# Reordering sums in a ring of buffers, moving a bias product into the first attention, and halving the last image's z: attention plus a non-local block on one Trainium2 core

## The chip, the core and the metric

The kernel runs on one core of a Trainium2 chip. The metric is device time in microseconds (us), the median over runs of the same program. Five engines work side by side, each through its own instructions in order: TensorE (PE in the profile, its weight loads PEld), VectorE (DVE), ScalarE (ACT), GpSimd (POOL) and SyncE (SP), which here only issues DMAs. They wait for one another through semaphores.

## The reference

The input x is 8 images of 512 channels and 32 x 32 positions, float32. The first layer is self-attention over positions with 8 heads of 64 channels and a residual; the second is a non-local block without a softmax, then a normalization over images and positions.

```python
# layer 0, per image: 512 channels, N = 1024 positions, 8 heads, d = 64
q, k, v = Wq@x + bq, Wk@x + bk, Wv@x + bv
attn = softmax(q_h^T k_h * d**-0.5)           # per head h
x1 = x + Wp@(attn v) + bp
# layer 1, C_INTER = 256
f = (theta@x1 + theta_b)(phi@x1 + phi_b)^T / N # 256 x 256
z = W@(f @ (g@x1 + g_b)) + W_b + x1
out = (z - mean) * rsqrt(var + eps) * gamma + beta   # over images and positions
```

Because the rows of a softmax add up to 1, the bias of v can be added after the projection: the kernel adds Wp@bv to bp once, and never to v.

## The kernel before

Channels lie on the 128 partitions in CC = 4 chunks, positions along the free axis, in float32 throughout. All projections are products of 2 x 2 blocks done with seven block products in place of eight (`seven`, L258; the table `SEVEN`, L220). For that, four differences of the data are needed per operand, named t1 to t4 (`more_sums`, L197), and four sums of the weights (`weight_sums`, L103). For q and k of images 1 to 7, and for the projection by Wp of images 1 to 6, some of the seven products are themselves done in seven smaller ones (`nested`, L240). Those need second-level differences of 128 x 256, held in one block per operand (`inner_parts`, L207): "inner 21" and "inner 22" from quarters of the data, "inner t4" from t4. For q and k they are used in the order 21, t4, 22 (L243, L244). The partial results of the smaller products sit in PSUM tiles named pq_in_s, pk_in_s, pp_in_s, which VectorE adds to the result (L319). TensorE accumulates the next small product on the same PSUM region, so it must wait for that addition.

A product with inner ones runs through numbered units, one 128 x 512 matmul each (16 of them in q and k). After a unit, `fills[unit]` calls a function of the caller (L303); so the caller places VectorE's work at points of TensorE's order. Instructions given to `dve`, `pe` or `sp` keep the program's order on their engine. All others are placed by a scheduler, which may move them ahead as far as their data and buffers allow.

Per image b the main loop (L801) runs: attention of image b; q, v and k of image b + 1, in this order; the projection by Wp of image b; theta and phi; then f, g, wf and z of the second layer. In the attention, scores are made 128 keys by 512 queries for two heads at once (L456), exponentiated by ScalarE into blocks e (L459), multiplied with v (L482) and added up by VectorE for the denominators (L465). `near_end` (L807) is called two steps before its end and prepares the differences of the next image's x. The denominators are folded together by DMAs that accumulate (`together`, L492) in a tile `fold` of 4 x 1024 per partition, then finished by a matmul, `den`, and a reciprocal (`all_denominators`, L520), after the second product of v (L836).

One ring of ten blocks of 128 x 1024 (`block`, L76) holds the e blocks, all differences t and inner blocks, and some weights. A new block can be written only when the last reader of the old one there is done. So the order in which blocks are asked for decides which old block each one waits for. In the phase of k, the differences of o (the attention's output) for the projection by Wp are made at `fills` 5, 7, 11 and 12, and its inner 21 at 13 and 14 (L840 to L843).

For image 0, `join_bias` (L174) makes Wp@bv: GpSimd scales and adds the quarters of Wp in SBUF after they are loaded, and four matmuls of one column (`pbp`, L187) add them over partitions, just before the projection.

z of the last three images (LATE = 3) is left for the end, because the statistics need all images. `last_z` (L747) goes over the four channel chunks oc. In each, `late_unit` (L726) makes z of an image for 1024 positions (4 matmuls), adds it to x1 and takes its statistics (`bn_stats`, L741), in two halves of 512 only for the last image of the last chunk. Then `begin` and `finish` aggregate the chunk's statistics, and all 8 images' chunk is normalized by ScalarE (in the last chunk by VectorE too) and written out by DMAs of 512 KB (L774). For chunk 0, z of the other late images was made earlier, so one image, number 7, is left.

Of the kernel before, what the change touches and what calls it, by code (L numbers as in the profile page):

```python
# [8 lines left out]
F32 = mybir.dt.float32  # L9
I32 = mybir.dt.int32  # L10
AF = mybir.ActivationFunctionType
ALU = mybir.AluOpType
# [4 lines left out]
P = 128  # L17
# [13 lines left out]
def unshifted(ctx: ExitStack, tc: tile.TileContext, a: dict, out: bass.AP):  # L31
    nc = tc.nc
    B, C, H, W = a["x"].shape
    N = H * W
    CC = C // P
# [26 lines left out]
    def pe(ins):  # L62
        tc.keep_in_program_order(ins)
# [8 lines left out]
    def next_bank(name):  # L72
        free.append(free.pop(0))
        return bank(free[-1], name)

    def block(name):  # L76
        return ring.tile([P, 2, 512], F32, tag="e", name=name)
# [93 lines left out]
        nc.sync.dma_start(kept[name][:, :14 * w.shape[3]], w.rearrange("p i k f -> p (i k f)"))  # L171
        nc.sync.dma_start(kept[name][:, 14 * w.shape[3]:], rest[name][:, :wide])

    def join_bias(w):  # L174

        t = w3.tile([P, 2, 512], F32, tag="acc", name="wp_bv")
        half = C // 2
        for m, quarters in enumerate(((w[:, 0], w[:, 1]), (corner["WpT"], w[:, 2]))):
            to, one = (t[:, i, m * half:(m + 1) * half] for i in range(2))
            for c in range(CC):  # L180
                nc.gpsimd.tensor_scalar(one if c else to, quarters[c // 2][:, c % 2, :], bv[:, c:c + 1], 1.0,
                                        ALU.mult, ALU.mult)
                if c:
                    nc.gpsimd.tensor_tensor(to, to, one, ALU.add)
        ps = next_bank("pbp")[:, 0, :CC]
        for oc in range(CC):
            pe(nc.tensor.matmul(ps[:, oc:oc + 1], t[:, 0, oc * P:(oc + 1) * P], ones, start=True, stop=True,  # L187
                                skip_group_check=True))
        nc.vector.tensor_tensor(bp, bp, ps, ALU.add)

# [6 lines left out]
    def more_sums(data, which, pin=lambda ins: None):  # L197
        for i in which:
            l, r = {1: ("12", "11"), 2: ("22", "t1"), 3: ("22", "12"), 4: ("21", "t2")}[i]
            data[f"t{i}"] = block(f"t{i}_{data['name']}")  # L200
            pin(nc.vector.tensor_tensor(data[f"t{i}"], data[l], data[r], ALU.subtract))

    def inner_sums(data, which, pin=lambda ins: None):
# [226 lines left out]
    def attention(b, q, k, v, near_end, make_f=None):  # L430
# [88 lines left out]

        def all_denominators(ps):  # L520

            t = folded.pop("t")[:, 2, :]
            columns(ps, folds8, lambda j: t[:, j * 512:(j + 1) * 512])
            ri = t[:, :512]
            nc.vector.reciprocal(ri, ps)
            d = dram2.tile([16, 512], F32, tag="den", name=f"den_d_{b}")
            nc.sync.dma_start(d, ri.rearrange("(a s) n -> a s n", a=16)[:, 0, :])
            d = d.rearrange("(j g i) n -> g j (i n)", j=2, g=2)
            return d[0], d[1]
# [36 lines left out]
        for i in range(len(steps) + LAG):  # L566
            if i < len(steps):
                scores(i)
            if make_f and i == 2:
                make_f(bank(tags[2], f"pf_{b - 1}"))  # L570
            if i in ((len(steps) - 5, len(steps) - 3) if make_f else (len(steps) - 2,)):
                near_end()
            if i >= LAG:
                weighted(i - LAG)
            if make_f and i == 46:
                first_den = denominators(0, bank(tags[2], f"den_{b}_0")[:, 0, :])
        free[:] = tags
# [169 lines left out]
    def last_z():  # L747
        order = [B - LATE, B - 1, *range(B - LATE + 1, B - 1)]
        for oc in range(CC):
            for n, b in enumerate(order if oc else [B - 1]):  # L750
                for h0, h1 in ((0, 1), (1, 2)) if (oc, n) == (CC - 1, LATE - 1) else ((0, NH),):
                    late_unit(b, oc, h0, h1)
            finish(oc, *begin(oc))

# [46 lines left out]
    for b in range(B):  # L801
        last = b == B - 1
        nxt = {}
        if not last:
            nxt["x"] = load_x(b + 1)

        def near_end():  # L807
            if not last:
                nxt["data"] = data_sums(quarters_of(nxt["x"]), f"x_{b + 1}", (1, 2))
                inner_sums(nxt["data"], "22", dve)  # L810
            elif "data" not in nxt:
                nxt["data"] = data_sums(quarters_of(held["x"]), f"x1_{b - 1}_again", (1,))
            elif "t2" not in nxt["data"]:
                more_sums(nxt["data"], (2,))
            else:
                more_sums(nxt["data"], (3, 4), dve)

        def held_f(ps):
            held["f"] = make_f(b - 1, held["tp"], ps)

        o, denominators, normalize = attention(b, q, k, v, near_end, held_f if last else None)
        between = None
        if not last:
            inner_sums(nxt["data"], "21", dve)
            later, of_t4 = [], []
            fills = {4: lambda: more_sums(nxt["data"], (3,), dve),
                     5: lambda: (more_sums(nxt["data"], (4,), dve), of_t4.extend(inner_parts(nxt["data"], "t4", dve))),
                     6: lambda: (of_t4[0](), of_t4[1]()), 7: lambda: (of_t4[2](), of_t4[3]())}
            q, peak_q = heads_of(b + 1, "q", weights("WqT"), bq, nxt["data"], dve, inner="WqT",
                                 later=later, fills=fills)  # L830
            load_w(nc.sync)

            def norm():
                nxt["products"] = normalize(denominators(next_bank(f"den_{b}")[:, 0, :]))

            v = values(b + 1, weights("WvT"), nxt["data"], {1: norm, 2: lambda: [one() for one in later], 5: lambda: nxt["products"]()})  # L836
            load_w(nc.sync)

            nxt["o"], of_21 = data_sums(quarters_of(o), f"o_{b}", ()), []
            fills = {unit: lambda i=i: more_sums(nxt["o"], (i,), dve) for unit, i in ((5, 1), (7, 2), (11, 3), (12, 4))}  # L840
            if b:
                fills[13] = lambda: (of_21.extend(inner_parts(nxt["o"], "21", dve)), of_21[0](), of_21[1]())
                fills[14] = lambda: (of_21[2](), of_21[3]())  # L843
            later_k = []
            k, peak_k = heads_of(b + 1, "k", weights("WkT"), bk, nxt["data"], later=later_k, inner="WkT",
                                 fills=fills)
            if b:
                inner_sums(nxt["o"], "t4", dve)
            load_w(nc.sync)
        else:  # L850
            nonlocal_(b - 1, held["x"], nxt["data"], held["f"], weights("WgT"), lambda: None,
                      {3: lambda: nxt.update(d=denominators(next_bank(f"den_{b}_1")[:, 0, :]))})
            z[b - 1] = [held["x"][:, cc, :] for cc in range(CC)]
            between = {4: late_unit(b - 1, 0, sums_now=False)}
            normalize(nxt["d"])()
            load_w(nc.sync)
            put_away(b - 1)
            for i, tag in enumerate("vqk"):
                reload(i, mats, tag)
            reload(3, foldp, "fold")  # L860
        w = weights("WpT")
        if b == 0:
            join_bias(w)
        project(b, xt, o, w, between, nxt.get("o"))
        if b == 0:
            keep_inner("WpT", w)
        load_w(nc.sync)
        if b == B - LATE:
            for cc in range(CC):
                nc.sync.dma_start(spill[b][:, cc, :], xt[:, cc, :])  # L870
        data = data_sums(quarters_of(xt), f"x1_{b}", (1, 2, 3, 4) if last else (1, 2))
        if last:
            reload_chunks(B - LATE)
        elif b > B - LATE and b != B - 2:
            z[b] = [xt[:, cc, :] for cc in range(CC)]
        tp = theta_phi(b, weights("tp"), data, {} if last else
                       {1: lambda: [one() for one in later_k[:2]], 2: lambda: [one() for one in later_k[2:]],
                        4: lambda: bound_scores(b + 1, q, k, peak_q, peak_k)})
        load_w(nc.sync)

        def before_wf():
            if last:
                late_unit(B - LATE, 0)
                z[b] = [xt[:, cc, :] for cc in range(CC)]
                reload(4, mats, "o")
                take_back(B - LATE + 1)

        if last:
            take_back(B - LATE)
        if b == B - 2:  # L890
            held.update(x=xt, tp=tp)
        else:
            nonlocal_(b, xt, data, lambda ps: make_f(b, tp, ps), weights("WgT"), before_wf)
            load_w(nc.sync)
            if b in spill_g:
                put_away(b)
        xt = nxt.get("x")
# [221 lines left out]
```

## Time and profile before

| what | value |
|---|---|
| median of 4 runs | 2154.0 us (2153.84 to 2154.33) |
| the profiled execution, its own time | 2154.0 us |
| its span, first to last instruction | 2152.3 us |
| granted TensorE clock | 0.996 |
| TensorE matmul busy | 2126.3 us, 99% of the span |
| VectorE busy | 1398.8 us, 65% |
| ScalarE busy | 746.4 us, 35% |
| GpSimd busy | 205.1 us, 10% |
| attention of image 0 begins, of image 1, of image 2 | 78.8, 345.8, 609.9 us |
| last matmul of the last z | about 2131 us |

The page lists, for each engine, its busy time, and for each group of instructions the line of the kernel, what it writes and reads, its count, and the mean duration of one. The chain of waits goes back from the last instruction to what released each step. The timeline lists instructions in order of time, merged where like ones follow each other, with the idle time ahead of them and what ended it. A matmul of 128 x 512 in float32 is two entries, and starts 0.86 us before the next one; the durations in the entries overlap, so starts are compared with starts.

### The profile page before, as it was taken

How to read it: one execution, taken by the hardware profiler on the slowest of the kernel's cores; microseconds unless marked ns; L12 is line 12 of the kernel's file. 1: busy time of each engine (PE TensorE's matmuls, PEld its weight loads, DVE VectorE, ACT ScalarE, POOL GpSimd, SP SyncE). 2: the span in 40 equal slices, each digit the busy share in tenths (PEclk: the TensorE clock that was granted, in tenths of full speed). 3: DMA queues.
4: the chain of work that ended last, by engine and by line, in shares of the span. 5: the costliest groups of instructions: out<-in, count | busy, mean ns of one | idle time of the engine just before them, and what ended most of it. 6: DMA issues, size and time to landing. Idle time of an engine off the chain costs nothing.

```text
span 2152.3 us, 30084 instructions
## 1 busy us (share of the span) xinstructions
PE 2126.3 (99%) x12510; PEld 1121.7 (52%) x12510; DVE 1398.8 (65%) x1690; ACT 746.4 (35%) x854; POOL 205.1 (10%) x256
## 2 busy tenths in 40 slices
PE   9999999999999999999999999999999999999996
PEld 4534664356733567335663366633666347643462
DVE  6466756667576675766657666576674675756736
ACT  1464104641046310463105621056212652056116
POOL 0111100110001100011000100011000110001000
PEclk9999999999999999999999999999999999999998
DMA  6333443334143331433324342233434234122758
GB/s 221 136 47 61 142 155 125 50 70 129 72 130 48 80 116 72 133 50 81 109 95 115 48 100 96 99 106 50 107 139 151 40 48 139 52 60 38 225 199 340
DMA packets 53375, 229.97 MB, mean 107 GB/s; under 512 B 9712, under 2 KB 16112, under 8 KB 45680
## 3 DMA queue, kind: packets, MB, share of 16 engines
q1 hardware_dynamic: 41552, 198.21, 27.2%
q0 software_dynamic: 10192, 28.46, 11.0%
q8 instruction: 100, 1.64, 0.3%
q10 hardware_dynamic: 1488, 1.32, 0.2%
q14 instruction: 43, 0.35, 0.1%
HBM read 140.79 MB, written 46.27 MB: 87 GB/s over the span
## 4 chain that ended last, share of the span: by engine, by line
PE 94%; DVE 2%; ACT 1%; DMA 1%; issue 1%; DVEq 0%; ACTq 0%
PE ps L456 20%; PE po L482 20%; PE pv L295 9%; PE ptp L295 9%; PE pp L295 7%; PE pq L295 5%; PE pg L295 4%; PE pk L295 4%; PE pq_in_s L250 3%; PE pf L622 3%; PE pz L295 2%; PE pk_in_s L250 2%; PE pp_in_s L250 2%; PE pwf L657 1%; DVE k L319 1%; ACT z L773 1%
## 5 line engine op out<-in xcount | busy, mean ns | idle before, releaser
L459 ACT ACTIVATE e<-ps 128x1024 f32<-128x1024 f32 x512 | 522.8, 1025 | 432.2 <-PE ps L456 426.7
L465 DVE TENSOR_TENSOR acc<-acc,e 128x1024 f32<-128x1024 f32 x384 | 469.9, 1224 | 144.6 <-ACT e L459 141.3
L482 PE MATMUL po<-e,v 64*64 64x512 f32 x4096 | 528.7, 589 | 0.7 <-ACT w_WgT L624 0.7
L456 PE MATMUL ps<-q,k 64*64 64x512 f32 x4096 | 529.1, 589 | 0.0
L482 PEld LDWEIGHTS po<-e,v 64*64 64x64 f32 x4096 | 156.5, 133 | 283.4 <-issue 275.7
L456 PEld LDWEIGHTS ps<-q,k 64*64 64x64 f32 x4096 | 155.6, 133 | 284.1 <-issue 275.0
L495 POOL DMA_DIRECT2D fold<-acc x189 | 147.2, 779 | 984.4 <-DMA fold<-acc 574.6
L463 DVE TENSOR_TENSOR acc<-e,e 128x1024 f32<-128x1024 f32 x64 | 78.3, 1224 | 143.7 <-ACT e L459 143.7
L645 ACT ACTIVATE g<-pg,gb 128x512 f32<-128x512 f32 x31 | 21.3, 687 | 410.6 <-PE pg L295 410.5
L295 PE MATMUL pv<-w_WvT,t_x 128*128 128x256 f32 x512 | 116.4, 381 | 0.0
L295 PE MATMUL ptp<-w_tp,t_x 128*128 128x256 f32 x512 | 114.4, 379 | 0.0
L295 PEld LDWEIGHTS pv<-w_WvT,t_x 128*128 128x128 f32 x512 | 96.6, 190 | 18.5 <-issue 5.7
L411 ACT COPY v<-pv 128x1024 f32<-128x1024 f32 x32 | 32.4, 1013 | 212.8 <-PE pv L295 212.8
L295 PEld LDWEIGHTS ptp<-w_tp,t_x 128*128 128x128 f32 x512 | 97.3, 190 | 13.2
L295 PE MATMUL pp<-t_o,w_WpT 128*128 128x512 f32 x208 | 100.8, 592 | 0.0
L295 PE MATMUL pq<-t_x,w_WqT 128*128 128x512 f32 x200 | 99.9, 593 | 0.6 <-DVE w_WqT L784 0.6
L423 POOL TENSOR_SCALAR q<-q,gates 128x1024 f32<-128x1024 f32 x32 | 35.2, 1113 | 680.5 <-DVE gates L421 587.3
L295 PE MATMUL pk<-t_x,w_WkT 128*128 128x512 f32 x200 | 100.0, 592 | 0.0
L295 PE MATMUL ptp<-w_tp,x 128*128 128x256 f32 x384 | 87.4, 381 | 0.0
L295 PE MATMUL pv<-w_WvT,x 128*128 128x256 f32 x384 | 86.8, 379 | 0.0
L319 DVE TENSOR_TENSOR k<-k,pk_in_s 128x256 f32<-128x256 f32 x119 | 48.3, 419 | 55.9 <-PE pk_in_s L250 41.5
L319 DVE TENSOR_TENSOR q<-q,pq_in_s 128x256 f32<-128x256 f32 x119 | 48.5, 420 | 51.1 <-PE pq_in_s L250 48.4
(179 smaller groups left out, 2306.4 us busy)
## 6 DMA issues: line engine op xcount, KB each, us to landing
fold<-acc POOLq DMA_DIRECT2D x189, 128.0 KB, 3.1
w_WqT<-kept_WqT SPq DMA_DIRECT2D x7, 2368.0 KB, 8.8
w_WkT<-kept_WkT SPq DMA_DIRECT2D x7, 2368.0 KB, 8.9
r<-den_d SPq DMA_DIRECT2D x32, 512.0 KB, 7.2
x<-in_x_dram SPq DMA_DIRECT2D x31, 512.0 KB, 5.8
w_WpT<-kept_WpT SPq DMA_DIRECT2D x6, 2176.0 KB, 8.3
w_WvT<-kept_WvT SPq DMA_DIRECT2D x7, 1792.0 KB, 7.1
w_tp<-kept_tp SPq DMA_DIRECT2D x7, 1792.0 KB, 7.3
```

Source lines behind the costliest of these rows:

```text
L250: pe(nc.tensor.matmul(ps, a[wi], d[di], start=s not in begun, stop=True, skip_group_check=True))
L295: pe(nc.tensor.matmul(to_ps, lhsT(k), rhs(k), start=(s, at) not in begun, stop=(k == nk - 1), skip_group_check=True))
L319: pin(nc.vector.tensor_tensor(at, at, ps if len(ps.shape) == 3 else ps.unsqueeze(1), ALU.add))
L411: seven(f"pv_{b}", w, data, True, lambda q, ps: nc.scalar.copy(at(q), as_v(ps)), lambda q, ps: dve(nc.vector.tensor_tensor(at(q), at(q), a ...
L423: nc.gpsimd.tensor_scalar(q[:, p, :], q[:, p, :], gate[:, p:p + 1], 1.0, ALU.mult, ALU.mult)
L456: pe(nc.tensor.matmul(ps[c * P // 2:(c + 1) * P // 2, j, :], k[r, p, keys], q[r, p, h * 512:(h + 1) * 512], start=True, stop=True, skip_gr ...
L459: nc.scalar.activation(e, ps, AF.Exp, scale=SCALE)
L463: nc.vector.tensor_tensor(accs[u], es[u, 0], e, ALU.add)
L465: ins = nc.vector.tensor_tensor(accs[u], accs[u], e, ALU.add)
L482: pe(nc.tensor.matmul(ps[j * D:(j + 1) * D, r, :], v[keys, m, (2 * p + j) * D:(2 * p + j + 1) * D], e[keys, j, :], start=(m == 0), stop=(m ...
L495: nc.gpsimd.dma_start(to, part_of, accum_op=ALU.add)
L622: pe(nc.tensor.matmul(ps[:, c, :], tp[:, i, c * P:(c + 1) * P], tp[:, i, CI:], start=(i == 0), stop=(i == NB - 1)))
```

## The change

Three parts.

1. Ring order. `near_end` asks for the block of t2 before that of t1, and makes inner 21 of the next x there instead of inner 22. Inner 22 is made in the phase of q, at units 8 and 9, its block asked for at unit 4. In the phase of k, t3 and t4 of o move from units 11 and 12 to 10 and 11, and its inner 21 from 13 and 14 to 12 and 14.
2. Bias. `join_bias` no longer takes the loaded quarters of Wp. It loads the four chunks of Wp anew into the unused fourth part of the tile `fold` of image 0's attention, by four DMAs on SP's queue, and VectorE scales and adds them, one `tensor_scalar` and three `scalar_tensor_tensor` of 128 x 512. None of the eight is pinned to an order. The four matmuls of one column stand just ahead of `den` of image 0, in the other half of its PSUM tile.
3. Last z. In `last_z`, the last image of every chunk is made in two halves of 512 positions; in chunk 0 that is image 7, the only one.

```diff
-    def join_bias(w):
-
-        t = w3.tile([P, 2, 512], F32, tag="acc", name="wp_bv")
-        half = C // 2
-        for m, quarters in enumerate(((w[:, 0], w[:, 1]), (corner["WpT"], w[:, 2]))):
-            to, one = (t[:, i, m * half:(m + 1) * half] for i in range(2))
-            for c in range(CC):
-                nc.gpsimd.tensor_scalar(one if c else to, quarters[c // 2][:, c % 2, :], bv[:, c:c + 1], 1.0,
-                                        ALU.mult, ALU.mult)
-                if c:
-                    nc.gpsimd.tensor_tensor(to, to, one, ALU.add)
-        ps = next_bank("pbp")[:, 0, :CC]
+    def join_bias(t):
+
+        t = t.rearrange("p (a n) -> p a n", a=2)
+
+        def get(c, to):
+            return lambda: nc.sync.dma_start(t[:, to, :], turned["WpT"][:, c, :])
+
+        def more(c):
+            return lambda: nc.vector.scalar_tensor_tensor(t[:, 0], t[:, 1], bv[:, c:c + 1], t[:, 0], ALU.mult, ALU.add)
+
+        return {9: get(0, 0), 10: get(1, 1), 14: lambda: nc.vector.tensor_scalar(t[:, 0], t[:, 0], bv[:, 0:1], 1.0,
+                                                                               ALU.mult, ALU.mult),
+                15: more(1), 17: get(2, 1), 22: more(2), 25: get(3, 1), 30: more(3)}
+
+    def bias_product(t, ps):
         for oc in range(CC):
-            pe(nc.tensor.matmul(ps[:, oc:oc + 1], t[:, 0, oc * P:(oc + 1) * P], ones, start=True, stop=True,
+            pe(nc.tensor.matmul(ps[:, oc:oc + 1], t[:, oc * P:(oc + 1) * P], ones, start=True, stop=True,
                                 skip_group_check=True))
         nc.vector.tensor_tensor(bp, bp, ps, ALU.add)
...
-            t = folded.pop("t")[:, 2, :]
+            t = folded.pop("t")
+            if b == 0:
+                bias_product(t[:, 3, :], ps[:, 1, :CC])
+            t, ps = t[:, 2, :], ps[:, 0, :]
...
+            if b == 0 and i == 8:
+                aside = join_bias(folded["t"][:, 3, :])
+            if b == 0 and i > 8 and i in aside:
+                aside[i]()
...
-            for n, b in enumerate(order if oc else [B - 1]):
-                for h0, h1 in ((0, 1), (1, 2)) if (oc, n) == (CC - 1, LATE - 1) else ((0, NH),):
+            images = order if oc else [B - 1]
+            for b in images:
+                for h0, h1 in ((0, 1), (1, 2)) if b == images[-1] else ((0, NH),):
...
-                nxt["data"] = data_sums(quarters_of(nxt["x"]), f"x_{b + 1}", (1, 2))
-                inner_sums(nxt["data"], "22", dve)
+                nxt["data"] = data_sums(quarters_of(nxt["x"]), f"x_{b + 1}", ())
+                nxt["data"]["t2"] = block(f"t2_x_{b + 1}")
+                more_sums(nxt["data"], (1, 2))
+                inner_sums(nxt["data"], "21", dve)
...
-            inner_sums(nxt["data"], "21", dve)
-            later, of_t4 = [], []
-            fills = {4: lambda: more_sums(nxt["data"], (3,), dve),
+            later, of_22, of_t4 = [], [], []
+            fills = {4: lambda: (of_22.extend(inner_parts(nxt["data"], "22", dve)),
+                                 more_sums(nxt["data"], (3,), dve)),
                      5: lambda: (more_sums(nxt["data"], (4,), dve), of_t4.extend(inner_parts(nxt["data"], "t4", dve))),
-                     6: lambda: (of_t4[0](), of_t4[1]()), 7: lambda: (of_t4[2](), of_t4[3]())}
+                     6: lambda: (of_t4[0](), of_t4[1]()), 7: lambda: (of_t4[2](), of_t4[3]()),
+                     8: lambda: (of_22[0](), of_22[1]()), 9: lambda: (of_22[2](), of_22[3]())}
...
-                nxt["products"] = normalize(denominators(next_bank(f"den_{b}")[:, 0, :]))
+                nxt["products"] = normalize(denominators(next_bank(f"den_{b}")))
...
-            fills = {unit: lambda i=i: more_sums(nxt["o"], (i,), dve) for unit, i in ((5, 1), (7, 2), (11, 3), (12, 4))}
+            fills = {unit: lambda i=i: more_sums(nxt["o"], (i,), dve) for unit, i in ((5, 1), (7, 2), (10, 3), (11, 4))}
             if b:
-                fills[13] = lambda: (of_21.extend(inner_parts(nxt["o"], "21", dve)), of_21[0](), of_21[1]())
+                fills[12] = lambda: (of_21.extend(inner_parts(nxt["o"], "21", dve)), of_21[0](), of_21[1]())
                 fills[14] = lambda: (of_21[2](), of_21[3]())
...
-        if b == 0:
-            join_bias(w)
         project(b, xt, o, w, between, nxt.get("o"))
```

In `more_sums`, a block is asked for only if the caller hasn't done so.

More of the change, by code (lines that the diff above doesn't have):

```diff
@@ L199, in more_sums @@
             l, r = {1: ("12", "11"), 2: ("22", "t1"), 3: ("22", "12"), 4: ("21", "t2")}[i]
-            data[f"t{i}"] = block(f"t{i}_{data['name']}")
+            if f"t{i}" not in data:
+                data[f"t{i}"] = block(f"t{i}_{data['name']}")
             pin(nc.vector.tensor_tensor(data[f"t{i}"], data[l], data[r], ALU.subtract))
```

## The prediction

> **What bounds the kernel now.** I read the page's busy times first, then the chain of waits, then TensorE's timeline where the change acts, with VectorE's beside it.
>
> ```profile
> PE 2126.3 (99%) x12510; PEld 1121.7 (52%) x12510; DVE 1398.8 (65%) x1690; ACT 746.4 (35%) x854; POOL 205.1 (10%) x256
> PE 94%; DVE 2%; ACT 1%; DMA 1%; issue 1%; DVEq 0%; ACTq 0%
> ```
>
> TensorE sets the end. The change removes no matmul of weight, so it can win only where TensorE waits, and behind its last matmul. The first such place is the end of each k phase, here image 1:
>
> ```profile
> 525.57 1.02 PE L295 MATMUL pk<-t_x,w_WkT 128*128 128x512 f32 x2
> 526.73 0.70 PE L250 MATMUL pk_in_s<-i_x,w_WkT 128*128 128x256 f32 x2
> 527.26 1.02 PE L295 MATMUL pp<-o,w_WpT 128*128 128x512 f32 x2
> ...
> 523.80 1.22 DVE L201 TENSOR_TENSOR t_o<-o,t_o 128x1024 f32<-128x1024 f32 x1
> 524.93 1.22 DVE L319 TENSOR_TENSOR k<-k,pk 128x1024 f32<-128x1024 f32 x1
> 526.25 0.42 DVE L319 TENSOR_TENSOR k<-k,pk_in_s 128x256 f32<-128x256 f32 x1
> ```
>
> Two entries of 128x512 take 0.86, so the last small product was due at 525.57 + 0.86 = 526.43. It came at 526.73, just behind the VectorE addition of 526.25. It lost 0.30, and 0.10 more in restarting (0.53 to the next start in place of 0.43). The same 0.40 stands at 790.8, 1054.8, 1318.8, 1582.9 and 1834.4. VectorE was late because t3, t4 and a large addition came in a row, though it had idled 1.96, 0.87 and 1.37 us shortly before.
>
> Image 0 has the same loss and, behind it, the bias product:
>
> ```profile
> 260.51 0.70 PE L250 MATMUL pk_in_s<-i_x,w_WkT 128*128 128x256 f32 x2
> 261.05 0.95 PE L187 MATMUL pbp<-ones,wp_bv 128*128 128x1 f32 x8
> 262.30 1.13 PE L295 MATMUL pp<-o,w_WpT 128*128 128x512 f32 x2 [0.31 <-DVE k L319]
> ...
> 242.84 0.87 DVE L106 TENSOR_TENSOR w_WpT<-a_WpT,w_WpT 128x512 f32<-128x512 f32 x1
> 243.64 0.68 DVE L106 TENSOR_TENSOR w_WpT<-w_WpT,a_WpT 128x512 f32<-128x512 f32 x1
> ```
>
> At the tail, the chain goes through ScalarE, but the windows show what drains last: DMA moves at its full rate, about 400 GB/s, from 2109 to 2148. It is fed too slowly only at first.
>
> ```profile
> 2106.00:2109.00 3.00, 3.00 (x8) 1.33 (x7) 2.83 (x4) 3.00 (x4) 0.00 (x0) 1.00 0.78 298
> 2109.00:2116.00 7.00, 7.00 (x17) 3.04 (x16) 5.83 (x11) 6.32 (x8) 0.00 (x0) 1.00 1.02 404
> 2137.00:2148.00 11.00, 0.00 (x0) 0.00 (x0) 1.51 (x3) 3.17 (x3) 0.00 (x0) 0.50 1.02 402
> ```
>
> So the end moves with the first output's start, as long as the queue never runs dry.
>
> **What the Trainium skill says.** "SBUF — State Buffer", Terms: VectorE and GpSimd share a port pair, held for a whole instruction, and the loser blocks. The trace agrees: beside GpSimd's bias work one weight sum of 128x512 took 0.87 and one 1.23, against 0.68 elsewhere. "TensorE: Matmul & The Clock Gate", Step-by-step: matmuls stay in program order, so one late addition holds all behind it, as at 526.73. "DMA: Bandwidth & Descriptors", Anatomy of one DMA, gives a fixed cost of about 2 us plus the bytes, on another issue path. Here the 256 KB loads of Wv were used 2.9 us after issue; I use 3.
>
> **Part 1, ring order.** No instruction is added; per image four second-level sums move from just behind the attention into the q phase, four sums of o move one unit ahead.
> In k of image 1 I refill VectorE's order with the trace's steps (0.34 for 128x256, 1.14 for 128x1024). t3 goes into the idle time before 521.11 (519.66 to 520.80), its block t2 of x being free after unit 9. t4 takes t3's place (521.81 to 522.94). Then two additions (to 523.80), one inner sum (524.14), the large addition (525.28), one inner sum (525.62), and the addition TensorE waits for, done at 526.04. That is 0.39 before 526.43. The inner sums of o now take the old inner 21, last read at unit 7, in place of inner 22, read until unit 15, so no wait comes with them. What is late next is the first use of pp in PSUM: two reads end at about 532.5, before the third product at about 535.5. Gain 0.40 for each of images 1 to 6: 2.4.
> In q, inner 22 (four times 0.34) falls at 467.2 to 467.9 and 470.2 to 470.9, where VectorE idled 2.18 and 0.87; unit 11 needs it at about 472.2. TensorE didn't wait in q before, so the gain is 0. If that cover were gone, up to 1.4 per image.
>
> **Part 2, bias.** At the projection of image 0, what goes is 0.29 + 0.10 (as in part 1), 1.25 from pbp to pp, and 0.10 of restart in pp (1.13 for 1.02): 1.74. The same eight entries come ahead of den: (0.95 - 0.25)/7 = 0.10 each, 0.85 with the entry. The addition to bp (0.15) delays the reciprocal, which nothing waited for. Net gain 0.9.
> Without GpSimd, the weight sum at 242.84 is 0.2 shorter; the small product of 245.63 was held 0.39 by the addition behind it. Bounds 0.1 and 0.6 for that stretch; I take 0.25.
> The cost lies where the diff doesn't show it. The eight unpinned instructions are moved by the scheduler to the very start: on VectorE ahead of the sums of the first q, on SP ahead of and between the stores of Wq's sums and the loads of Wv. The trace has no such scaling from SBUF; by the rows of 128x1024 tensor_scalar (0.81) and 128x512 two-input sums (0.68) I take 0.42 and 0.68.
> The line, by the start's timeline. SP issues chunks 0 and 1 at about 18.9 and 19.4, behind 2.25 MB whose data end near 24.5, so they land at 25.5 to 26.5. VectorE scales at 26.1 and adds until 27.2; it idled 0.89 before 27.01, so 0.2 is lost. Chunk 2 is issued at 27.3, lands near 30.2, and its addition ends at 30.9; the q sums, peaks and weight sums that follow end near 37.1 (36.2 before). Only then SP can store the rest of Wq's sums (30.55 before). That lands at about 41, the loads of Wv are issued then (37.16 before), and the first sum of Wv, standing at the head of VectorE's queue, starts near 44 (40.06 before). The additions to k behind it slip: the one of 47.61 ends at about 49.5. TensorE's last k product, at 50.84, needs its region. So 1.3 us of cover remain; Wv itself is needed only at 54.44. Cost 0, and each microsecond of lateness beyond 1.3 costs one.
>
> **Part 3, last z.** In chunk 0 the first half is ready 1.72 after 2096.90, at 2098.65; its addition (0.76 to the next start) and statistics end at 2100.1, before the second half's matmuls do. From 2100.38 only 0.76 + 0.72 follow, so the aggregation starts at 2101.86 and not at 2103.01: 1.15. In chunks 1 and 2 the same gives 0.65, as the first half queues behind the image before it. The output thus starts 1.15 earlier, but chunk 1's output (2115.76 before) only 0.65. Chunk 0 is 4.19 MB; drained by the windows' rates it ends near 2117.1, when chunk 1's had flowed for about 0.7. With half of that cover gone, some 0.3 is lost in refilling. Bounds 0.65 and 1.15; I take 0.85.
>
> **Sum.** 2.4 + 0.9 + 0.25 + 0.85 = 4.4. The span of 2152.3 becomes 2147.9; the profiled execution took 2154.0, equal to the median, so 2149.6.
>
> **Rivals.** *A: a part of it is hidden anyway.* The tail yields 0.65 or nothing, or a next wait takes some of the k phases: the cover there is only 0.39. For it: margins of tenths in each. Against: the k arithmetic uses the trace's own steps. Gain 2 to 3.5: 2150.5 to 2152.
> *B: the moved bias stalls the start.* Place: the last k product of image 0, then Wv. It decides once the line above is late by more than 1.3, and the kernel is slower than before from 1.3 + 4.4 = 5.7. For it: five DMA landings in a row, each blocking SP or VectorE in order, in slices where DMA is busy. Against: between 24 and 30 us DMA was nearly idle. At 9 us late, 7.7 is lost: 2149.6 + 7.7 = 2157.3; at 12 us, 2160.
> *C: more is won*: the tail in full (+0.3) and all of image 0's held stretch (+0.4), perhaps some q waits: 2148.9 or below, to 2148.2.
>
> **How the numbers follow.** Forecast 0.57, with its own range 2149.0 to 2150.2; A 0.18; B 0.15, two thirds of it beyond the old time; C 0.10. The range runs from C's end, 2148.2, through A to 2152.4, leaving out most of B. What a measurement of this kernel can tell from no change is about 0.2%, 4.3 us, so the border lies at 2149.7, in the middle of the forecast. Faster: 0.33 of the forecast and C, 0.43. Same: 0.24 of it, A and 0.04 of B, 0.46. Slower: 0.11 of B.
>
> **What would show it.** Right: pp of image 1 follows pk_in_s without the 0.30 hold, in all six images; no pbp ahead of pp in image 0, and four one-column matmuls at den; the sum of 242.84 back at 0.68; the aggregation of chunk 0 about 1.15 nearer to its matmuls; the last k product of image 0 without idle time before it. Wrong: idle TensorE near 50 us; DMA below its full rate near 2116 (A), or a new hold in q or k.

## The result, and the profile after

| | before | after |
|---|---|---|
| median of all runs | 2154.02 us (58 runs, 2153.25 to 2155.52) | 2150.77 us (38 runs, 2150.04 to 2151.93) |
| the profiled execution | 2154.0 us | 2151.27 us |
| its span | 2152.3 us | 2149.6 us |

The ratio of the times is 0.9985, with an interval from 0.998 to 0.9989. The change won 3.25 us where 4.4 were forecast: 0.15%, less than the 0.2% at which the prediction drew its line between faster and no change. 2150.77 lies outside the forecast's own range, 2149.0 to 2150.2, and inside that of rival A. In the pair of profiled runs, whose account follows, the places that the forecast named won 3.9 us, and 1.2 were given back at others. The profiled run of after is 0.5 slower than the median.

The page of after begins with the busy times; the second line is the chain of waits.

```profile
PE 2124.2 (99%) x12510; PEld 1122.3 (52%) x12510; DVE 1402.5 (65%) x1697; ACT 746.6 (35%) x854; POOL 193.4 (9%) x242
PE 96%; ACT 1%; DVE 1%; DMA 1%; issue 0%; SPq 0%; DVEq 0%; ACTq 0%
```

GpSimd lost its 14 instructions and 12 us. VectorE has 4 of the 7 new ones from the bias, 3 from the halves. In the chain, TensorE went from 94% to 96%, VectorE from 2% to 1%: some of the waits for VectorE are gone from it.

TensorE's timeline at the end of the k phase of image 1:

```profile
524.69 1.02 PE L299 MATMUL pk<-t_x,w_WkT 128*128 128x512 f32 x2
525.55 0.59 PE L254 MATMUL pk_in_s<-i_x,w_WkT 128*128 128x256 f32 x2
525.98 1.88 PE L299 MATMUL pp<-o,w_WpT 128*128 128x512 f32 x4
```

The small product comes 0.86 after the two entries ahead of it and is followed after 0.43: neither hold nor restart. Images 2 to 6 look the same. The gain of five images, from the first product of q of image 2 to that of image 7, is 1307.71 - 1305.69 = 2.02, five times 0.40; the sixth is 0.39 (259.21 to 258.82, up to the projection of image 7).

In image 0, the bias product stands ahead of den, and the projection follows its k phase directly:

```profile
217.81 1.03 PE L299 MATMUL pv<-w_WvT,t_x 128*128 128x256 f32 x4
218.67 0.95 PE L190 MATMUL den<-ones,fold 128*128 128x1 f32 x8
219.87 1.08 PE L432 MATMUL den<-fold,folds 128*64 128x512 f32 x4 [0.25 <-DVE bp L192]
...
261.10 0.59 PE L254 MATMUL pk_in_s<-i_x,w_WkT 128*128 128x256 f32 x2
261.53 2.74 PE L299 MATMUL pp<-o,w_WpT 128*128 128x512 f32 x6
```

The bracket is what the forecast missed: den waits 0.25 for the addition to bp, so it comes 219.87 - 218.67 = 1.20 behind the first of the eight entries, and not 0.85. Counted from the start of the sixteen entries of pv ahead of both, den comes after 3.55 before and after 4.65 now: a net cost of 1.10.

At the head of the projection of image 7 there is a wait that the profile before did not have. There VectorE multiplies o by r, the reciprocals of the softmax denominators. Half of them at a time is written to `den_d` in DRAM (16 KB) and loaded back as r, spread over the partitions (1 MB): two DMAs, one behind the other. First before, then after, TensorE and VectorE:

```profile
2022.69 5.79 PE L295 MATMUL pp<-o,w_WpT 128*128 128x512 f32 x13
2024.79 2.36 DVE L562 TENSOR_TENSOR o<-o,r 128x1024 f32<-128x1024 f32 x2 [3.42 <-DMA r<-den_d]
```

```profile
2019.40 3.60 PE L299 MATMUL pp<-o,w_WpT 128*128 128x512 f32 x8
2023.56 2.84 PE L299 MATMUL pp<-o,w_WpT 128*128 128x512 f32 x6 [0.56 <-DVE o L569]
2022.28 2.36 DVE L569 TENSOR_TENSOR o<-o,r 128x1024 f32<-128x1024 f32 x2 [3.93 <-DMA r<-den_d]
```

The first of the two late products of o with r began 2024.79 - 2022.69 = 2.10 after the projection before, 2.88 after it now. It takes 1.14, and TensorE needs the result four products of 0.86 in, at 3.44. The limit is therefore near 2.3: the kernel before was 0.2 inside it, after is 0.6 outside.

At the end, DMA in windows (the columns are the length, then busy time and instructions of TensorE, its weight loads, VectorE, ScalarE and GpSimd, the granted clock, DMA's share, GB/s):

```profile
2111.00:2113.00 2.00, 2.00 (x6) 0.95 (x5) 1.77 (x4) 1.32 (x3) 0.00 (x0) 1.00 1.02 410
2113.00:2115.00 2.00, 2.00 (x6) 0.85 (x5) 1.30 (x3) 2.00 (x3) 0.00 (x0) 1.00 1.00 379
2115.00:2117.00 2.00, 2.00 (x6) 0.86 (x5) 1.85 (x2) 2.00 (x3) 0.00 (x0) 1.00 0.88 350
2117.00:2134.00 17.00, 11.93 (x30) 5.03 (x28) 15.36 (x30) 15.64 (x17) 0.00 (x0) 0.92 1.02 402
```

The rate dips to 350 after chunk 1's first output is issued, at 2112.65: that is the refilling which the prediction described, and the sign that it named for rival A.

The last lines are SP's waits behind the last output's issue (who waited for what, us in total, times, longest), before and then after:

```profile
SPq L26 <- SPq L26: 3.3, 4, 1.3
```

```profile
SPq L26 <- SPq L26: 3.5, 1, 3.5
```

At the end SP waits in turn for eight completion semaphores, the counters that tell it of a DMA's landing. Before, the last landing stood fifth in its list, and three waits followed it; in after it stands first, and the other seven follow. From that landing to the last of the eight waits the trace has 0.20 before and 0.54 after; to the end of the span it has 1.88 and 2.23.

The account of the two profiled runs, in the order of time: start +0.07 (TensorE already stands 0.06 later at 13 us, ahead of anything that the change touches); image 0 -0.94; images 1 to 6 -2.41; projection of image 7 +0.78 (24.08 to 24.86); TensorE's wait between the two halves of z of image 7, at 2095.6, +0.08; first output nearer to TensorE's last product by 1.12; outputs, from the first issue to the last landing, longer by 0.47 (44.96 to 45.43); end +0.35. The sum is -2.72, and the spans differ by 2.74.

### The profile page after: what moved, and what is told of

It reads as the page before. It is cut to its first block, busy times and chain, and to the rows that moved or that the text cites. A ratio compares the mean times of both kernels' runs of the same rounds, so it can differ in the third digit from the quotient of the medians.

```text
span 2149.6 us, 30078 instructions
## 1 busy us (share of the span) xinstructions
PE 2124.2 (99%) x12510; PEld 1122.3 (52%) x12510; DVE 1402.5 (65%) x1697; ACT 746.6 (35%) x854; POOL 193.4 (9%) x242
## 4 chain that ended last, share of the span: by engine, by line
PE 96%; ACT 1%; DVE 1%; DMA 1%; issue 0%; SPq 0%; DVEq 0%; ACTq 0%
PE ps L460 21%; PE po L486 20%; PE pv L299 9%; PE ptp L299 9%; PE pp L299 7%; PE pk L299 6%; PE pq L299 5%; PE pg L299 4%; PE pk_in_s L254 3%; PE pq_in_s L254 3%; PE pf L633 3%; PE pz L299 2%; PE pp_in_s L254 2%; PE pwf L668 1%; ACT z L785 1%; PE pz L744 1%
```

## The experiments

Every kernel was timed beside the kernel before; "against before" is the difference of the medians in the same series. The series ran on several chips, and the median of the kernel before lay between 2154.02 and 2154.48 in them; so the expectations, which are absolute times, are best read against it. The four middle columns are read from the timelines and SP's waits: image 0, from the first product of q of image 1 to that of image 2; the projection of image 7, whose length without a hold is 24.03; from the first output's issue to the last landing; from there to the end.

| kernel | image 0 | projection 7 | outputs | end | profiled run | against before | ratio, interval |
|---|---|---|---|---|---|---|---|
| before | 266.98 | 24.08 | 44.96 | 1.88 | 2154.0 | | |
| after | 266.04 | 24.86 | 45.43 | 2.23 | 2151.27 | -3.25 | 0.9985 (0.998 to 0.9989) |
| ring alone | 267.05 | 24.14 | 44.98 | 1.88 | 2151.94 | -2.10 | 0.9989 (0.9983 to 0.9996) |
| bias alone | 266.45 | 24.09 | 44.99 | 2.73 | 2153.95 | +0.80 | 1.0003 (0.9995 to 1.0011) |
| last z alone | 267.57 | 24.37 | 45.54 | 1.88 | 2154.29 | -0.58 | 0.9998 (0.999 to 1.0007) |
| bias pinned | 266.04 | 24.64 | 45.58 | 2.73 | 2151.66 | -2.84 | 0.9986 (0.9979 to 0.9993) |
| later loads | 266.04 | 24.69 | 45.34 | 2.22 | 2150.82 | -3.52 | 0.9984 (0.9977 to 0.9991) |
| half chunk 0 | 266.04 | 24.33 | 46.15 | 2.23 | 2151.19 | -2.93 | 0.9987 (0.998 to 0.9993) |
| bias alone, four DMAs | 266.45 | 24.52 | 44.78 | 2.30 | 2153.72 | -0.72 | 0.9997 (0.9989 to 1.0005) |
| after, four DMAs | 266.04 | 24.03 | 45.05 | 2.25 | 2149.95 | -4.62 | 0.9978 (0.997 to 0.9987) |
| r on another queue | 266.04 | 24.69 | 45.37 | 2.23 | 2150.68 | -3.42 | 0.9984 (0.9978 to 0.9991) |
| before, r on another queue | 267.47 | 24.75 | 44.98 | 1.88 | 2154.79 | +0.17 | 1.0001 (0.9992 to 1.0009) |
| after, eight DMAs | 266.04 | 24.45 | 45.37 | 2.60 | 2151.01 | -3.37 | 0.9985 (0.9978 to 0.9991) |
| spare buffer alone | 266.04 | 24.64 | 45.17 | 2.24 | 2150.34 | -4.07 | 0.998 (0.9973 to 0.9988) |

**Each part alone.** Three kernels, each the kernel before with one part of the change as the diff above has it; their cores:

```diff
ring alone:
-                inner_sums(nxt["data"], "22", dve)
+                inner_sums(nxt["data"], "21", dve)
...
bias alone:
-        if b == 0:
-            join_bias(w)
...
last z alone:
+                for h0, h1 in ((0, 1), (1, 2)) if b == images[-1] else ((0, NH),):
```

> The kernel before with part 1 alone. Theory T (the forecast's sizes for parts 1 and 2 hold; what is missing in the whole change is a new hold at the projection of image 7, the products of o with r, 0.83, and some tenths behind the last output): the six holds of 0.40 go, 2154.0 - 2.4 = 2151.6. Whether the hold of image 7 comes here too is open: if part 1's earlier arrival there brings it, 2151.6 + 0.8 = 2152.4, and the profile has pp waiting for o at the head of image 7's projection. Rival P (the parts overlap or undo each other, nothing is wrong at image 7): 2151.6, and the three parts alone add up to more than the whole change by about 1.

> The kernel before with part 2 alone. Theory T: image 0 becomes shorter by 0.9 as in the profile of the changed kernel, nothing else moves: 2154.0 - 0.9 = 2153.1. The forecast had 1.15: 2152.85. Rival S (the start line of chunk loads and stores costs something in other runs than the profiled one): 2153.5 to 2154.5, with TensorE idle near 50 us or at the first product of v.

> The kernel before with part 3 alone. Theory T: the data of the outputs end 0.87 earlier, as in the profile of the changed kernel, and what lies behind the last landing is chance: 2154.0 - 0.87 = 2153.15. Rival R (the queue runs dry ahead of chunk 1's output and the end of the last DMA costs 0.3 more): 2153.5 to 2153.7.

Ring alone won 2.10, 0.3 less than theory T. In its profile five of the six images are 0.40 shorter. The sixth lost 0.35 in the q phase of image 3, where an addition of VectorE came 0.35 later against TensorE's products than in after, and TensorE was held by those behind it. So the cover in q can be used up, though in after it wasn't. Image 7 has 0.11 of hold. The part does what was said, and by itself brings no hold to image 7. In image 0 part 1 alone moves the loss rather than removing it: the small product of k is no longer held, and behind the bias product pp idles.

```profile
260.81 0.95 PE L187 MATMUL pbp<-ones,wp_bv 128*128 128x1 f32 x8
262.18 2.84 PE L296 MATMUL pp<-o,w_WpT 128*128 128x512 f32 x6 [0.43 <-DVE k L320]
```

Bias alone was a miss: 0.80 slower, past both theories, though the interval of the ratio reaches down to 0.9995, which is about the expected -0.9. Its one profile shows the gain in image 0 and no hold at the start or in image 7, but 0.85 more at the end (1.88 to 2.73). It was the fastest of 13 runs; about 1 us of the others' time is not shown by it. It does show a step that the prediction booked in the wrong place: without part 1 the hold of 0.30 at the end of k of image 0 stays.

```profile
259.78 1.02 PE L298 MATMUL pk<-t_x,w_WkT 128*128 128x512 f32 x2
260.94 0.70 PE L253 MATMUL pk_in_s<-i_x,w_WkT 128*128 128x256 f32 x2
```

Last z alone won 0.58, near rival R's value. Its first output comes 1.12 nearer to TensorE's last product, and the outputs take 0.58 longer. Its profile also lost 0.59 in image 0, where GpSimd's bias work lengthened one of VectorE's sums from 1.21 to 1.78 and TensorE stood there for 0.47:

```profile
245.49 1.78 DVE L201 TENSOR_TENSOR t_o<-o 128x1024 f32<-128x1024 f32 x1
247.66 0.70 PE L250 MATMUL pk_in_s<-i_x,w_WkT 128*128 128x256 f32 x2 [0.47 <-DVE k L319]
```

The same 1.78 stands in "before, r on another queue". In both, a sum of GpSimd had begun 0.02 before VectorE's (245.47 and 245.49 here); in the profile of before it began 0.07 after it, and VectorE took 1.21. This fits the shared port pair of the Trainium skill, which one engine holds for a whole instruction while the other blocks ("SBUF — State Buffer", Terms). It cost more in these runs than the one profile of before showed: with the bias on VectorE image 0 is the same to 0.01 in all eight profiles of the whole change; with it on GpSimd it varies by 0.6.

The parts don't add up: alone they win 2.10 - 0.80 + 0.58 = 1.88, together 3.25. Of the difference, 0.48 lies in image 0: there part 2 alone wins 0.53, part 1 alone loses 0.07, and both together win 0.94. The rest is not explained; bias alone, about 1 us slower than its profile, would account for it.

**The start.** The loads and sums of the bias are pinned to where the text has them:

```diff
-            return lambda: nc.sync.dma_start(t[:, to, :], turned["WpT"][:, c, :])
+            return lambda: sp(nc.sync.dma_start(t[:, to, :], turned["WpT"][:, c, :]))
...
-            return lambda: nc.vector.scalar_tensor_tensor(t[:, 0], t[:, 1], bv[:, c:c + 1], t[:, 0], ALU.mult, ALU.add)
+            return lambda: dve(nc.vector.scalar_tensor_tensor(t[:, 0], t[:, 1], bv[:, c:c + 1], t[:, 0], ALU.mult, ALU.add))
```

> The changed kernel with the four loads of the bias pinned on SP and its four sums pinned on VectorE where the text has them, inside the first attention; the start then runs as in the kernel before. Theory T: the start was covered, so nothing is won: 2150.8, between 2150.6 and 2151.0; the four sums of 128x512 beside the attention cost nothing, since VectorE idles there. Rival S (the start line costs some tenths): 2150.3 or less. The other way, if a sum late in the attention holds a score product: more than 2151.2.

It was no faster (-2.84 to after's -3.25), so the start was covered. The timelines agree: the last product of k of image 0 begins at 50.91 in after and at 50.88 here. Its 2151.37 lies in the range of "the other way", a held score product, but no such hold is seen: the q phase that follows the first attention begins at 188.83 here and at 188.86 in after. What its profile has more is at the end, 2.73 to 2.23. The cover in after was thin. VectorE, the sum of Wv, and then the additions that k needs:

```profile
44.47 0.69 DVE L106 TENSOR_TENSOR w_WvT<-w_WvT,a_WvT 128x512 f32<-128x512 f32 x1 [4.94 <-DMA w_WvT<-in_WvT_dram]
...
49.12 1.22 DVE L323 TENSOR_TENSOR k<-k,pk 128x1024 f32<-128x1024 f32 x1
```

It ended near 50.3, 0.6 ahead of TensorE.

**The hold in image 7, first attempt.** One DMA of 512 bytes on SP's queue holds back what was issued behind the loads of r:

```diff
             normalize(nxt["d"])()
+            sp(nc.sync.dma_start(dram.tile([P, 1], F32, tag="mark", name="mark"), o[:, CC - 1, N - 1:]))
             load_w(nc.sync)
```

> The changed kernel with one more DMA of 512 bytes on SP, behind the loads of r of image 7, that reads the last normalized element of o: so SP issues the loads of Wp's successor weights, the stores of g and the loads of z only after r has been used, about 7.5 later. Theory D (the loads of r land late because 1.8 MB and more behind them share the DMA engines; the hold is there in most runs): r is used 1 to 3 earlier, the hold of 0.72 at the head of image 7's projection goes, 2150.8 - 0.7 = 2150.1. Rival F (the two DMA round trips have their length whatever runs beside them, and the hold comes and goes from run to run): the profile may show it or not, time 2150.5 to 2150.9. Rival L (the later loads are needed soon): TensorE waits at theta and phi or in the last z, over 2151.

Theory D falls. The product of o with r began 2.71 after the projection's start (2.88 in after), and TensorE waited again:

```profile
2023.21 3.70 PE L299 MATMUL pp<-o,w_WpT 128*128 128x512 f32 x8 [0.39 <-DVE o L569]
```

So the loads behind r are not what delays it: here SP issued nothing else between r and its use. In the packets of the trace, the 16 KB of den_d move only when the 1 MB of r ahead of them (heads 0 to 3) is nearly through: in after that 1 MB ends 5.62 before the projection's start, and den_d's packets lie between 6.17 and 5.87 before it. That is 2.5 behind their issue, where the first packets of r follow theirs after 1.3.

**The hold, second attempt.** So the first two loads of r go to ScalarE's DMA queue, in the changed kernel and in the kernel before:

```diff
-        def rows_of(g, d):
+        def rows_of(g, d, q=nc.sync):
...
-                sp(nc.sync.dma_start(rows[g][j * D:(j + 1) * D, :], d[j].partition_broadcast(D)))
+                sp(q.dma_start(rows[g][j * D:(j + 1) * D, :], d[j].partition_broadcast(D)))
...
-                rows_of(0, first_den)
+                rows_of(0, first_den, nc.scalar)
```

> The changed kernel with the first two loads of r of image 7 (1 MB, heads 0 to 3) issued on ScalarE's DMA queue and not on SP's; the write of the second denominators then no longer stands behind them in SP's queue. Theory D2 (in image 7 the write of den_d starts only when the 1 MB of r ahead of it has landed, so the second loads of r come just at or behind the time at which the projection needs them, in most runs of the changed kernel behind it): r is used about 1 earlier, no hold at the head of image 7's projection, 2150.8 - 0.6 = 2150.2, between 2149.9 and 2150.4, and runs lie closer together. Rival F (the hold is rare and the profiled runs were unlucky): 2150.6 to 2150.9. Rival G (both queues share the same 16 engines, and den_d waits as long): the hold stays in the profile.

> The kernel before with the same two loads on ScalarE's DMA queue. Theory D2 with a hold that belongs to the changed kernel's runs: nothing to win here, 2154.2 within 0.2. If the kernel before has the hold in most runs too, though its profiled run had none: 2153.6, and then the hold explains nothing of the shortfall.

Rival G holds. den_d's packets still start 2.2 behind their issue, the loads of r on SP follow after 3.91 (4.00 in after), and TensorE waits:

```profile
2010.42 0.59 SPq L548 DMA_DIRECT2D den_d<-ri  x1
2014.33 1.13 SPq L556 DMA_DIRECT2D r<-den_d  x2
2023.04 1.55 PE L299 MATMUL pp<-o,w_WpT 128*128 128x512 f32 x3 [0.39 <-DVE o L569]
```

The Trainium skill says that the issuing queues share the same 16 DMA engines, and that using several only saves issue time ("Trainium Kernel Development and Optimization", Key Constraints), and that an engine drains a whole packet of descriptors, 9 to 17 as a rule, from one ring before it turns to the next ("DMA: Bandwidth & Descriptors", Queues, rings and completion order). The 1 MB of r are 128 pieces of 8 KB in the trace; shared out evenly that is 8 for each of 16 engines, few enough for one or two such packets. The traces agree: in all fourteen profiles, in the two with the other queue as well, 112 or 113 of the 128 pieces were through before den_d's first packet. How the pieces are grouped they don't show, and no run leaves the 1 MB out. The kernel before has the hold too in this variant (24.75), at an unchanged time. Over all fourteen profiles the late product of o with r begins between 1.84 and 2.88 behind the projection's start; the hold is 0.5 on average in the eight of the whole change and its variants, 0.3 in the six others. That it belongs to the change is not shown. It is a chain of DMA round trips which ends near its limit of 2.3 in every version, from 0.5 inside it to 0.6 outside.

**The last z.** Halves in chunk 0 and the last chunk alone:

```diff
-                for h0, h1 in ((0, 1), (1, 2)) if b == images[-1] else ((0, NH),):
+                for h0, h1 in ((0, 1), (1, 2)) if b == images[-1] and oc in (0, CC - 1) else ((0, NH),):
```

> The changed kernel with the last image halved in chunk 0 and the last chunk alone; chunks 1 and 2 as before. Theory Q (the first output starts 1.1 earlier, but chunk 1's data come no earlier than in the kernel before, and the queue runs dry between them; what counts is chunk 1's start): the gain of part 3, some 0.6, goes back to 0 to 0.2: 2151.2 to 2151.4, and DMA is seen below its rate for about 1 us ahead of chunk 1's output. The forecast's picture (half a microsecond of cover in the queue): 0.3 to 0.5 of the gain stays, 2150.9 to 2151.1.

Theory Q holds in the profile. The first output comes as early as in after, the outputs take 46.15 from there, 0.72 more, and DMA falls below its rate:

```profile
2111.00:2113.00 2.00, 2.00 (x6) 0.94 (x5) 1.86 (x5) 1.32 (x3) 0.00 (x0) 1.00 0.92 365
2113.00:2115.00 2.00, 2.00 (x6) 0.81 (x6) 1.89 (x3) 2.00 (x3) 0.00 (x0) 1.00 0.70 262
```

Against before, the outputs start 1.12 earlier and last 46.15 - 44.96 = 1.19 longer: nothing is left. What counts is the start of chunk 1's output. Measured back from TensorE's last product it is issued at 15.43 before, 15.44 here and 16.11 in after: with all the halves 0.68 earlier, 0.60 once TensorE's own wait of 0.08 is taken off. Over the eight profiles with all the halves the outputs last 45.36 on average, 44.94 over the five without any, so the gain of part 3 is 1.12 - 0.42 - 0.08 = 0.62. The times don't decide: -2.93 is 0.3 short of after's -3.25, the intervals overlap, and 2154.02 - 2.93 = 2151.09 falls within the range of the forecast's picture.

**The end.** Four DMAs of 2 KB are added in the first attention, into a buffer that nothing reads, to turn the order of the eight completion semaphores back:

```diff
+    spare = const.tile([P, 4, CC], F32, tag="spare", name="spare")
...
+            if b == 0 and 40 <= i < 44:
+                sp(nc.sync.dma_start(spare[:, i - 40, :], a["bq"]))
```

> Part 2 alone, with four more DMAs of 2 KB on SP's queue in the first attention, into a buffer that nothing reads. The DMAs use eight completion semaphores in turn, and SP waits for all eight at the end; part 2's four DMAs shift which of them the last output has, so that seven waits follow its landing and not three. Theory E (this order is what makes part 2 alone slower): with eight more DMAs the order is that of the kernel before, the time from the last landing to the end goes from 2.66 back to about 1.8, and the time from 2155.0 to 2154.2, or 2153.1 if the profiled run's other numbers hold in all runs. Rival H (part 2 alone holds TensorE somewhere that its one profile didn't show, near image 7 or at the start): 2154.5 to 2155, and this profile may show where.

> The whole change with the same four DMAs of 2 KB. Theory E: SP's last waits have the order of the kernel before, three behind the landing and not seven, 0.34 less: 2150.4. Rival (the waits at the end have other reasons, or the order is not restored): 2150.6 to 2151.0.

Both became faster, by more than the order of the waits can give: bias alone went from +0.80 to -0.72, and the changed kernel from -3.25 to -4.62, with 12 runs between 2149.50 and 2150.07. On the same chip, all 20 runs of "later loads" were at 2150.60 or above. The order of SP's waits did turn back, here after with four DMAs:

```profile
SPq L26 <- SPq L26: 3.9, 4, 1.3
```

From the last landing to the last of the eight waits it is 0.20 again, as theory E said. But the end is no shorter for it, 2.25 to 2.23: SP now pauses for 0.38 a little later, which nothing in the profile explains. In the profile of after with four DMAs the gain lies elsewhere. Image 7 is not held, and the outputs take 45.05, not 45.43.

```profile
2019.28 4.88 PE L299 MATMUL pp<-o,w_WpT 128*128 128x512 f32 x11
2021.12 2.36 DVE L570 TENSOR_TENSOR o<-o,r 128x1024 f32<-128x1024 f32 x2 [3.30 <-DMA r<-den_d]
```

Two more kernels ask what the four DMAs changed: eight of them in place of four, with a buffer of 128 bytes on each partition and not 64, and the buffer of 64 bytes with a `memset` in place of the DMAs.

```diff
eight DMAs:
-    spare = const.tile([P, 4, CC], F32, tag="spare", name="spare")
+    spare = const.tile([P, 8, CC], F32, tag="spare", name="spare")
...
-            if b == 0 and 40 <= i < 44:
+            if b == 0 and 40 <= i < 48:
...
spare buffer alone:
-                sp(nc.sync.dma_start(spare[:, i - 40, :], a["bq"]))
+                dve(nc.vector.memset(spare, 0.0))
```

> The whole change with eight of the 2 KB DMAs in the first attention in place of four. Theory O (what the four gained, about 1, comes from the order of the eight completion semaphores): eight leave the order as in the changed kernel, so the time is back at 2150.8. Rival C (any shift of this sort moves the DMA round trips of image 7 and the end by some tenths to one, in either direction): 2149.8 to 2151.5, with the time of the last product of o with r and the hold behind it telling which.

> The whole change with the 64-byte buffer of the four small DMAs, but without the DMAs: VectorE writes the buffer once in the first attention. It tells apart what the four small DMAs changed. Theory O (the number of DMAs on SP's queue counts: it decides which of the eight completion semaphores each later DMA has): the time stays with the changed kernel's, 2150.7 to 2151.1. Rival A (the buffer shifts where all later tiles lie, and that is what made the transfers at the end and in image 7 shorter): 2149.8, with no hold at the head of image 7's projection and the data of the outputs ending earlier.

Eight gave -3.37, as theory O expects: the order of the semaphores is that of after again, and so is the time. The buffer alone gave -4.07, which theory O doesn't expect. Its own profile shows the hold of image 7 (24.64), the order of after and a start 0.54 earlier. That start is no sign of the buffer: it stands already at 13 us, ahead of the `memset`, and over all fourteen profiles the same point varies by as much (12.49 to 13.03). So neither the number of DMAs nor the place of the tiles is shown to be the cause, and the intervals of these ratios overlap. All three kernels with the buffer of 64 bytes were faster than their like without it, the one with 128 bytes was not; as eight DMAs came with the larger buffer, the two can't be told apart. What stays open is why programs that differ in such a trifle lie up to 1.4 us apart. The best time measured is that of the whole change with the four DMAs, 2149.82, ratio 0.9978 (0.997 to 0.9987); whether it is better than the change by itself isn't settled.

## Why the prediction was right, and where it fell short

- **Part 1, right in size.** 2.4 forecast, 2.41 in the profile. There, no wait appeared in q or k, and the inner sums of o brought none.
- **Part 2, right in kind, 0.2 too much.** Image 0 was to win 1.15 and won 0.94. The mis-sized term is the eight entries ahead of den: the prediction has 0.85 for them and says that the addition to bp delays only the reciprocal. They cost 1.20, because den waits for that addition. The trace names the addition; that den waits because it shares a PSUM tile with the bias product is read from the code, and no run tests it. Net it is 1.10, where the prediction has 0.85. The 0.40 at the end of k of image 0, booked under part 2, takes both parts. The freed stretch came out as said, 0.29 for 0.25: the weight sum lasts 0.68 in place of 0.87, the hold behind it fell from 0.39 to 0.20, and another 0.10 was won behind a second sum, 0.68 in place of 1.23. So 1.74 + 0.29 - 1.10 = 0.93, against the 0.94 that image 0 won.
- **The start, right at 0, with less cover.** 1.3 were forecast, 0.6 were left. The loads of Wv were issued at 41.65, as worked out, but the addition that TensorE needed ended at 50.3 and not 49.5. Rival B did not occur, and pinning the work won nothing.
- **Part 3, right in kind, too large.** 0.85 was a middle between two bounds. The profile of halved chunk 0 shows that the queue had no such cover: chunk 1's start decides, and the lower bound, 0.65, was the value to take. The pair of profiles gives 1.12 - 0.47 - 0.08 = 0.57.
- **The sum, short of two terms.** "What is late next" was answered at each place of the change, but not further down. Image 7's loads of r were 0.2 inside their limit in the profile of before, and cost 0.78 in the profiled run of after; the end behind the last landing cost 0.35. Neither is in the sum. With them, 2.41 + 0.94 + 0.57 - 0.78 - 0.35 - 0.07 (start) = 2.72, against 2.74 between the spans. All ten profiles with part 2 have at least 0.34 more at the end (2.22 to 2.73, against 1.88 in all four without it); the first comes and goes, and the runs don't show that it belongs to the change. Of the 1.15 between the forecast and the medians, 0.2 of part 2, 0.25 of part 3 and 0.35 at the end are thus accounted for; some 0.35 is not.

So rival A was nearer than the forecast, and the prediction is right because its range took A in. It said that a part is hidden or a next wait takes it, and gave 2150.5 to 2152, in which 2150.77 lies. It named the k phases and the tail: the tail was right, and the k phases kept all they won.

## What to carry to other kernels

When waits of 0.4 us are removed one by one, what they are worth is soon decided by chains that lie far from the change and already end at their limit: list every place where a DMA round trip lands within 0.3 us of its use, not only those that the diff touches. If an output stream has several bursts, an earlier first burst is worth only what the start of the next burst moves. Below about 0.1%, take several profiles of the same kind before a difference is given a cause: two programs with the same arithmetic lay 1.1 us apart here on one chip, and up to 1.4 across series.

## What the runs showed of the hardware

- A write of 16 KB that was issued 3.4 us after 1 MB of loads moved only when 112 or 113 of their 128 pieces were through, 2.0 to 2.7 us after its issue, in all fourteen profiles: twelve from the same issuing queue, two from another (2.2 and 2.5).
- A VectorE sum of 128x1024 took 1.78 us where a GpSimd sum had begun 0.02 us before it, and 1.21 us where that began 0.07 us after it.
- Four DMAs of 2 KB in the first attention went with 1.4 and 1.5 us less in two pairs of programs, eight of them with 0.1 less, a buffer without them with 0.8 less; the pairs were timed in different series. The cause is open.
- From the last landing to the end of the program it was 1.88 us in the four programs without part 2, 2.22 to 2.30 in seven with it and 2.60 to 2.73 in three. SP's eight waits took 0.20 us of it where the last landing stood fifth among them, 0.54 where it stood first. In five programs, all with part 2, a pause of 0.38 between two of SP's later instructions came on top; its cause is open.
